# Cross-attention over a long context: context read feature-major, the mean taken out of the weights, keys staged in DRAM, the rescaling factor spread by DMAs

## The chip, the cores and the metric

The kernel runs on one core of a Trainium2 chip. The core has a matrix engine (TensorE, PE in the profile, with PEld for its weight loads), a vector engine (VectorE, DVE), a scalar engine (ScalarE, ACT), a general engine (GpSimd, POOL) and a queue engine that only issues DMAs (SyncE, SP). Each engine works through its own queue in order, and the engines wait for each other by semaphores. The metric is the device time of one execution in microseconds.

## The reference

The model is one layer of a Perceiver: 512 latent rows of 512 features attend to a context of 8192 rows, and a stack of eight blocks and a routed feed-forward layer follow. Only the first part, the cross-attention, is touched by the change. Everything is float32.

```python
def layer_norm(x, g, b):
    mu = jnp.mean(x, axis=-1, keepdims=True)
    var = jnp.var(x, axis=-1, keepdims=True)
    return (x - mu) * jax.lax.rsqrt(var + EPS) * g + b

xn = layer_norm(x, gamma_x, beta_x)          # x: the context, 8192 x 512
ln = layer_norm(latents, gamma_l, beta_l)    # latents: 512 x 512
q = (ln @ Wq).reshape(b, m, h, d)            # 8 heads of 64
kv_x = xn @ Wkv
k_x, v_x = (kv_x[..., :INNER], kv_x[..., INNER:])
kv_l = ln @ Wkv                              # the latents are keys and values too
k_l, v_l = (kv_l[..., :INNER], kv_l[..., INNER:])
k_x = rope_rotate_k(k_x)                     # halves of each head turned by cos and sin of the position
...
k = jnp.concatenate([k_x, k_l], axis=2)      # 8704 keys
v = jnp.concatenate([v_x, v_l], axis=2)
attn = jax.nn.softmax(jnp.einsum('bhid,bhjd->bhij', q * scale, k), axis=-1)
out = jnp.einsum('bhij,bhjd->bhid', attn, v)
out = jnp.transpose(out, (0, 2, 1, 3)).reshape(b, m, INNER) @ Wo
...
x = x + cross_attention(ctx_1024, _layernorm(x), ...)
x = x + eight_blocks(_layernorm(x), ...)
x = x + routed_feed_forward(_layernorm(x), ...)
```

## The kernel before

The attention is computed with keys on the partitions and queries along the free axis. The 8704 keys are cut into 17 blocks of 512: block 0 is the latents themselves, blocks 1 to 16 are the context. A block is four chunks of 128 keys. The eight heads are four pairs.

**From context rows to keys and values.** `fetch_block` loads four row tiles of 128 x 512 and the cos and sin table of the block. `moments_of` (L176, L177, DVE) takes mean and variance of each row, `roots_of` the reciprocal root by three Newton steps on tiles of 4 columns (on POOL from block 3 on), and `centre` (L194, ACT) applies `r*x - r*mean` in place. `transpose_rows` (L218, PE) turns the tiles to features on partitions, 16 transposes a block, and its four evictions (L224, ACT) multiply by gamma and add beta. `keys_of(b, j)` multiplies four feature tiles with 128 columns of the key weights (L231); the weights' columns are permuted so that j even holds first halves of heads and j odd second halves. DVE multiplies the product by cos and sin (L249), POOL combines the halves (L254, L255), and eight DMAs on SP's queue (L262) place the 32-row pieces into two key tiles. `values_of(b, t)` (L231 too) makes the values of one chunk, evicted by ACT (L270).

**From keys to the output.** The work on scores is cut into 24 *units*. A unit is one pair of heads and a run of chunks: 4, 6, 9, 12, 12, then sixteen times 13, then 10, 7, 4. `score` makes two 128 x 512 products of one chunk (pc, L379), ACT copies them out of PSUM (L382), and DVE keeps the running maximum over chunks (mx, L386, L388). At the unit's end `maxima` transposes that maximum (pmx, L397), DVE reduces it and joins it with the pair's earlier maximum (mrow, L401), POOL subtracts old and new (alpha, L406), and ACT takes the exponential (L407): this is the factor by which the pair's earlier output must shrink. `maxima_rows` (mbc, L416) spreads the maximum over the partitions. `shrink` spreads alpha the same way by eight small products (pa, L427), and DVE multiplies the pair's accumulated output and sums with it (L432). `exponentials` subtracts on DVE (L439), takes the exponential on ACT (L440), and POOL adds the chunks up in one buffer (es, L448, L450). `weigh` multiplies with the values (po, L460), `sums` turns es into the denominators (pd, L499), and `gather` (L490) adds both into the pair's output. When a pair is done, `ones_over` multiplies by the reciprocal (L523), and `project` (L483) applies the output weights.

**What sets the order.** PE's order is the program's order, written out by hand (`manual_schedule`). Time is counted in *pairs of steps* d: each d makes the scores of two chunks, and `todo[d]` holds what else PE does in it, sorted by `rank`. A block takes 8 of these d, a unit of 13 chunks 6.5. The other engines and SP's queue are ordered by the framework's scheduler when the program is built. PSUM has five banks shared by scores, projections and transposes (`ps_s`, bufs 5); the score tiles in SBUF have 18 buffers, es has one. `queued(...)` keeps an operation from being put before a given one.

The opening, before d = 0, makes keys and values of block 1 and of block 0 and the queries. The tail projects, adds the residual, and opens the next stage, whose first weights SP loads (L131).

Of the kernel before, what the change touches and what calls it, by code (L numbers as in the profile page):

```python
# [13 lines left out]
PSUM = bass.MemoryType.PSUM  # L14
DRAM = bass.MemoryType.DRAM

P = 128
# [37 lines left out]
def perceiver_kernel(  # L55
    ctx: ExitStack, tc: tile.TileContext, x, cx, wq_x, wkv_x, wo_x, wq, wk, wv, wo, wf1, wf2,
# [81 lines left out]
    xnp = pool("x_feat", 4, stack=xa)  # L138
    cbp = pool("x_rows", 4, stack=xa)
    xpool = pool("xattn", 1, stack=xa)  # L140
    kvp = pool("x_kv", 27, stack=xa)
    sp = pool("x_s", 18, stack=xa)
# [69 lines left out]
    k_sb, v_sb, xT, part, rows_of, trigs = {}, {}, {}, {}, {}, {}  # L212

    def transpose_rows(b, dc, gcol, bcol):
# [4 lines left out]
        xT[b, dc] = xnp.tile([P, BLK], F32, tag="xn", name="xn")  # L219
        scale, shift = (col[:, c + dc : c + dc + 1] for c in (gcol, bcol))  # L220
        if b == 1 and dc % 2:
            nc.vector.tensor_scalar(xT[b, dc], pt, scale, shift, ALU.mult, ALU.add)
        else:
            nc.scalar.activation(xT[b, dc], pt, AF.Identity, bias=shift, scale=scale)  # L224
# [12 lines left out]
    def keys_of(b, j):  # L237
# [37 lines left out]
    def fetch_block(b):  # L275
# [1106 lines left out]
```

## Time and profile before

| | us |
|---|---|
| median of 3 runs (2569.86 to 2571.99) | 2571.08 |
| the profiled execution | 2571.29 |
| its span | 2569.2 |
| PE busy in the span | 2501.5 |
| DVE busy | 1746.6 |
| ACT busy | 1202.3 |
| POOL busy | 1263.4 |

The span is the time from the first to the last recorded instruction; 2.1 us of the execution lie outside it. The granted clock of TensorE was 0.995 on average. A group in the profile is named by line, engine and operation, then what it writes and reads with the shapes; `x` is the count, then busy time and the mean of one in nanoseconds, and behind the bar the idle time of the engine just before such instructions, with what ended it. PE's float32 products are recorded as two instructions each, transposes as one. In the timeline a row is a run of equal instructions: start, length, and in brackets the idle time before it.

### The profile page before, as it was taken

Reading aid. Unit: us, or ns where it says so; the run is one execution under the profiler, and the core shown is the slowest. Engines: PE = TensorE matmul, PEld = TensorE weight load, DVE = VectorE, ACT = ScalarE, POOL = GpSimd, SP = SyncE. Lnnn points to the kernel's source line nnn. Section 1 sums busy time; section 2 is a strip of 40 time slices with the busy share of each in tenths; the row PEclk is TensorE's granted clock in tenths of the full one; section 3 lists DMA queues with packets and bytes.
Section 4 is the critical chain, followed back from the end, with each engine's and each line's share of the span. In section 5 each row is a group of like instructions: output and inputs, shape, how many; then the busy total and the mean of one; then the engine's idle time right before and its main releaser. Section 6 shows DMA issues by size and latency. Waiting matters only on the chain.

```text
span 2569.2 us, 33740 instructions
## 1 busy us (share of the span) xinstructions
PE 2501.5 (97%) x11560; PEld 1471.0 (57%) x11560; DVE 1746.6 (68%) x3680; ACT 1202.3 (47%) x2285; POOL 1263.4 (49%) x1422
## 2 busy tenths in 40 slices
PE   8999999999999999998999999999999999999998
PEld 4433333334333333333588686886868878687764
DVE  4466767766777776886675767757576575766764
ACT  3465656665566665663433415334153441524303
POOL 0255665666567666775144452544525354263512
PEclk9999999999999999998999999999999999999999
DMA  3111111111111111010522223222222323223235
GB/s 134 42 44 52 29 41 42 42 40 43 34 42 41 42 42 42 9 42 17 193 95 93 72 79 106 95 95 70 95 95 90 95 86 97 92 74 99 66 110 203
DMA packets 98380, 187.49 MB, mean 73 GB/s; under 512 B 10336, under 2 KB 10464, under 8 KB 98208
## 3 DMA queue, kind: packets, MB, share of 16 engines
q1 hardware_dynamic: 88496, 167.29, 20.3%
q10 hardware_dynamic: 8688, 15.94, 2.0%
q0 software_dynamic: 1024, 2.10, 0.3%
q8 instruction: 92, 1.51, 0.2%
q14 instruction: 80, 0.66, 0.1%
HBM read 162.22 MB, written 1.05 MB: 64 GB/s over the span
## 4 chain that ended last, share of the span: by engine, by line
PE 78%; DVE 9%; ACT 5%; issue 4%; POOL 2%; DMA 0%; SPq 0%; DVEq 0%; POOLq 0%; ACTq 0%
PE pb L846 14%; PE ps L635 13%; PE pw L730 9%; PE pv L231 7%; PE pk L231 6%; PE ps L730 6%; PE po L460 6%; PE pc L379 6%; DVE sc L439 4%; PE po L1009 4%; ACT sc L382 2%; ACT sc L440 2%; DVE mx L388 1%; PE pt L218 1%; PE pf L939 1%
## 5 line engine op out<-in xcount | busy, mean ns | idle before, releaser
L450 POOL TENSOR_TENSOR es<-es,sc 128x1024 f32<-128x1024 f32 x222 | 526.1, 2370 | 110.5 <-ACT sc L440 99.9
L388 DVE TENSOR_TENSOR mx<-pc,mx 128x512 f32<-128x512 f32 x448 | 283.3, 684 | 186.5 <-ACT sc L382 186.3
L440 ACT ACTIVATE sc<-sc 128x1024 f32<-128x1024 f32 x272 | 288.4, 1065 | 249.2 <-DVE sc L439 238.1
L382 ACT COPY sc<-pc 128x512 f32<-128x512 f32 x544 | 284.4, 600 | 81.3 <-PE pc L379 67.6
L439 DVE TENSOR_TENSOR sc<-sc,mbc 128x1024 f32<-128x1024 f32 x272 | 319.4, 1209 | 3.7 <-PE mbc L416 2.2
L379 PE MATMUL pc<-qT,k 64*128 64x512 f32 x1088 | 290.9, 621 | 5.8 <-DVE sin L249 2.3
L460 PE MATMUL po<-sc,v 128*64 128x512 f32 x1088 | 263.0, 604 | 0.2 <-DVE mx L388 0.2
L231 PE MATMUL pk<-xn,wkv 128*64 128x512 f32 (+1 forms) x856 | 250.6, 604 | 8.2 <-ACT v L270 3.4
L231 PE MATMUL pv<-wkv,xn 128*64 128x512 f32 (+1 forms) x808 | 248.0, 598 | 7.7 <-DVE sin L249 2.6
L379 PEld LDWEIGHTS pc<-qT,k 64*128 64x128 f32 x1088 | 101.4, 186 | 189.0 <-issue 80.9
L1019 ACT ACTIVATE h<-h,col 128x256 f32<-128x256 f32 x192 | 103.9, 577 | 220.5 <-DVE h L779 151.0
L903 ACT ACTIVATE g<-g 128x512 f32<-128x512 f32 x64 | 39.9, 630 | 344.7 <-DVE g L863 218.7
L730 PE MATMUL pw<-curT,cur 128*128 128x256 f32 (+1 forms) x896 | 177.3, 350 | 0.1
L231 PEld LDWEIGHTS pk<-xn,wkv 128*64 128x64 f32 (+1 forms) x856 | 85.0, 153 | 160.8 <-issue 114.1
L231 PEld LDWEIGHTS pv<-wkv,xn 128*64 128x64 f32 (+1 forms) x808 | 86.6, 155 | 150.8 <-issue 110.8
L812 POOL TENSOR_TENSOR sh<-h 128x128 f32<-128x128 f32 x120 | 83.4, 695 | 176.7 <-PE pb L846 172.1
L986 POOL TENSOR_TENSOR y<-qf,y 128x512 f32<-128x512 f32 x32 | 44.5, 1391 | 243.9 <-DVE y L985 243.9
L730 PEld LDWEIGHTS pw<-curT,cur 128*128 128x128 f32 x896 | 150.2, 190 | 16.9 <-DVE curT L723 0.2
L863 DVE TENSOR_TENSOR g<-g,pb 128x256 f32<-128x256 f32 x135 | 50.0, 417 | 159.7 <-PE pb L846 159.2
L717 POOL TENSOR_TENSOR cur<-w 128x256 f32<-128x256 f32 x128 | 93.5, 741 | 118.5 <-DVE g L904 74.9
L460 PEld LDWEIGHTS po<-sc,v 128*64 128x64 f32 x1088 | 73.6, 138 | 135.2 <-issue 120.0
L846 PE MATMUL pb<-tw,sh 128*128 128x256 f32 x540 | 136.2, 379 | 0.0
(220 smaller groups left out, 4639.7 us busy)
## 6 DMA issues: line engine op xcount, KB each, us to landing
w<-in_wf SPq DMA_DIRECT2D x64, 1024.0 KB, 5.2
k<-cos SPq DMA_DIRECT2D x272, 64.0 KB, 2.0
cb<-in_cx SPq DMA_DIRECT2D x62, 256.0 KB, 3.9
row<-in_rows ACTq DMA_DIRECT2D x48, 256.0 KB, 4.7
f<-in_f SPq DMA_DIRECT2D x10, 1024.0 KB, 5.3
tg<-in_trig SPq DMA_DIRECT2D x16, 512.0 KB, 3.6
wk<-in_wk SPq DMA_DIRECT2D x8, 1024.0 KB, 5.2
wq<-in_wq SPq DMA_DIRECT2D x8, 1024.0 KB, 5.1
```

The source lines that it names most:

```text
L231: nc.tensor.matmul(ps[o : o + n, :], lhs(dc)[:, o : o + n], rhs(dc), start=(dc == 0), stop=(dc == DC - 1))
L379: nc.tensor.matmul(pc[h], k_sb[b, p][hs, o : o + P], qT[hs, p, :], start=True, stop=True)
L382: copied[0] = nc.scalar.copy(sc[:, h, :], pc[h])
L388: behind[0] = nc.vector.tensor_tensor(mx[u][:, h, :], pc[h], mx[u][:, h, :], ALU.max)
L439: nc.vector.tensor_tensor(sc, sc, mbc[u], ALU.subtract)
L440: nc.scalar.activation(sc, sc, AF.Exp)
L450: nc.gpsimd.tensor_tensor(es[u], es[u], sc, ALU.add)
L460: nc.tensor.matmul(po[u][h * HD : (h + 1) * HD, :], v_sb[b, p][:, t * P + h * HD : t * P + (h + 1) * HD], scores[u, i][:, h, :], start=(i ...
L635: nc.tensor.matmul(ps[:, t0 : t0 + n], w[:, dc, c0 : c0 + P], xT[:, dc, t0 : t0 + n], start=(dc == 0), stop=(dc == DC - 1),)
L730: nc.tensor.matmul(ps, lhs[:, k], rhs[:, k], start=(k == 0), stop=(k == 1))
L846: nc.tensor.matmul(ps[i], lhs, rhs, start=(q == 0 and i in (1, 2, 6, 5, 4)), stop=(q == self.N - 1 and i in (1, 2, 7, 3, 4)),)
L1019: nc.scalar.activation(h, h, AF.Gelu_apprx_tanh, bias=col[:, c : c + 1])
```

## The change

The context is sent a second time, transposed (`cxt`, features by rows). `fetch_features` loads a block of it as four feature tiles, so blocks 2 to 16 need no `transpose_rows` and no `centre`; the row tiles are still loaded, for their moments only. The layer norm is taken apart:

- The factor r of each row: `spread_roots` writes the 512 reciprocals to DRAM and reads them back on all partitions, and `scale_tokens` multiplies the four feature tiles with them, on POOL (for block 2 half on DVE).
- The mean: with gamma multiplied into the weights and the column's mean taken off (`column_means`, PE; `centre_weights`, DVE), the product of a raw row is the product of its centred row. This is done once, in the opening, when block 1 and block 0 have used the weights as they are.
- The shift beta becomes a bias: `beta_of` multiplies it with the weights, one column at a time. For keys the bias is added in the multiplication by cos and sin; for values it is added at the end, times the sum of the weights, in `ones_over`. Block 0's values are made from `xT - beta` so that the one bias holds for all.

Keys go to DRAM in two tiles per two products (POOL's queue issues these writes from block 2 on) and `load_keys` brings them back for each unit and block, two d ahead, on SP's queue. Alpha's subtraction moves from POOL to DVE; `factor` transposes alpha (PE), takes the exponential (ACT), and writes it to DRAM, from where two DMAs spread it; the units of `spread_here` (21, 22, 23) keep the products of before. The shrinking is put at `end + 4` where the DMAs spread, and stays at `end + 2` in the others. Pools: feature tiles 2 of 8 KB a partition (4 of 2 KB before), key and value tiles 15 (27), 4 tiles of loaded keys, score tiles 19 (18).

```diff
-    xnp = pool("x_feat", 4, stack=xa)
+    xnp = pool("x_feat", 2, stack=xa)
-    kvp = pool("x_kv", 27, stack=xa)
-    sp = pool("x_s", 18, stack=xa)
+    kvp = pool("x_kv", 15, stack=xa)
+    ktp = pool("x_k", 4, stack=xa)
+    sp = pool("x_s", 19, stack=xa)
+    dram = pool("x_dram", 1, DRAM, stack=xa)
...
+        if b > 1:
+            roots[b] = r, None
+            return
...
+    def spread_roots(b):
+        line = dram.tile([TT, P], F32, name=f"r{b}")
+        nc.sync.dma_start(out=line.rearrange("t p -> p t"), in_=roots[b][0])
+        spread[b] = xpool.tile([P, BLK], F32, tag="rbc", name="rbc")
+        nc.sync.dma_start(out=spread[b], in_=line.rearrange("t p -> (t p)").partition_broadcast(P))
+    def scale_tokens(b, dc):
+        x = xT[b, dc]
+        eng = nc.vector if b == 2 and dc % 2 else nc.gpsimd
+        eng.tensor_tensor(x, x, spread[b], ALU.mult)
     def normalizing(b):
-        yield from ((1 + t // 2, moments_of, b, t) for t in range(TT))
+        yield from ((t // 2, moments_of, b, t) for t in range(TT))
-        yield from ((6 + t // 2, centre, b, t) for t in range(TT))
+        if b < 2:
+            yield from ((6 + t // 2, centre, b, t) for t in range(TT))
+        else:
+            yield (4, spread_roots, b)
+            yield from ((6 + dc // 2, scale_tokens, b, dc) for dc in range(DC))
...
-    def transpose_rows(b, dc, gcol, bcol):
+    bias = xpool.tile([P, 2, DC], F32, name="bias")
+    g_d = xpool.tile([P, DC], F32, name="g_d")
+    early = ps_o.tile([P, 2, DC], F32, tag="o", name="early")
+    def transpose_rows(b, dc, dst, gcol, bcol):
-        xT[b, dc] = xnp.tile([P, BLK], F32, tag="xn", name="xn")
-        scale, shift = (col[:, c + dc : c + dc + 1] for c in (gcol, bcol))
+        xT[b, dc] = dst
+        scale = col[:, gcol + dc : gcol + dc + 1]
+        shift = 0.0 if bcol is None else col[:, bcol + dc : bcol + dc + 1]
         if b == 1 and dc % 2:
-            nc.vector.tensor_scalar(xT[b, dc], pt, scale, shift, ALU.mult, ALU.add)
+            nc.vector.tensor_scalar(dst, pt, scale, None, ALU.mult)
+        elif bcol is None:
+            nc.scalar.activation(dst, pt, AF.Copy, scale=scale)
         else:
-            nc.scalar.activation(xT[b, dc], pt, AF.Identity, bias=shift, scale=scale)
+            nc.scalar.activation(dst, pt, AF.Identity, bias=shift, scale=scale)
+    def beta_of(i, j):
+        for dc in range(DC):
+            nc.tensor.matmul(
+                early[:, i, j : j + 1], wkv[:, i, dc, j * P : (j + 1) * P],
+                col[:, C_BX + dc : C_BX + dc + 1], start=(dc == 0), stop=(dc == DC - 1),
+            )
+        nc.vector.tensor_copy(bias[:, i, j : j + 1], early[:, i, j : j + 1])
+    def column_means(i):
+        for dc in range(DC):
+            nc.tensor.matmul(
+                means[:, i, :], g_d[:, dc : dc + 1].to_broadcast([P, P]), wkv[:, i, dc, :],
+                start=(dc == 0), stop=(dc == DC - 1),
+            )
+    def centre_weights(i):
+        for dc in range(DC):
+            w = wkv[:, i, dc, :]
+            nc.vector.scalar_tensor_tensor(
+                w, w, col[:, C_GX + dc : C_GX + dc + 1], means[:, i, :], ALU.mult, ALU.subtract
+            )
     def projected(ps, lhs, rhs):
...
-                nc.vector.tensor_tensor(part[c + str(half)], pk, trigs[b][:, i, :], ALU.mult)
+                nc.vector.scalar_tensor_tensor(
+                    part[c + str(half)], pk, bias[:, 0, j : j + 1], trigs[b][:, i, :], ALU.add, ALU.mult
+                )
-        for p in (j - 1, j):
-            k_sb[b, p] = kv_tile(f"k{b}_{p}")
-            for h in range(2):
-                src = slice((p % 2 * 2 + h) * H2, (p % 2 * 2 + h + 1) * H2)
-                for i, half_of in enumerate((lo, hi)):
-                    o = h * HD + i * H2
-                    nc.sync.dma_start(out=k_sb[b, p][o : o + H2, :], in_=half_of[src, :])
+        k_dr[b, j // 2] = dram.tile([2, P, BLK], F32, name=f"k{b}_{j // 2}")
+        for i, half_of in enumerate((lo, hi)):
+            (nc.gpsimd if b > 1 else nc.sync).dma_start(out=k_dr[b, j // 2][i], in_=half_of)
+    def load_keys(u, b, lo, hi):
+        kt[u, b] = ktp.tile([P, BLK], F32, tag="kt", name=f"kt{u}_{b}")
+        p = units[u][0]
+        for h in range(2):
+            o = (p % 2 * 2 + h) * H2
+            nc.sync.dma_start(
+                out=kt[u, b][h * HD : (h + 1) * HD, lo:hi], in_=k_dr[b, p // 2][:, o : o + H2, lo:hi]
+            )
     def values_of(b, t):
-        projected(pv, lambda dc: xT[b, dc][:, t * P : (t + 1) * P], lambda dc: wkv[:, 1, dc, :])
+        projected(pv, lambda dc: xT[b if b else "v", dc][:, t * P : (t + 1) * P], lambda dc: wkv[:, 1, dc, :])
...
-    def fetch_block(b):
+    def fetch_rows(b):
...
+    def fetch_turns(b):
+    def feature_tiles(b, tiles):
+        for dc in range(DC):
+            xT[b, dc] = tiles[dc]
+    def fetch_features(b):
+        t = xnp.tile([P, DC, BLK], F32, tag="xn", name="xn")
+        nc.sync.dma_start(out=t, in_=cxt[:, (b - 1) * BLK : b * BLK].rearrange("(c p) t -> p c t", p=P))
+        feature_tiles(b, [t[:, dc, :] for dc in range(DC)])
     def normalize_block(b):
...
     def fetch_weights(i):
-    fetch_block(1)
+    fetch_rows(1)
+    fetch_turns(1)
+    spare = {}
+    for b in (1, "v"):
+        spare[b] = []
+        for _ in range(2):
+            t2 = sp.tile([P, 2, T], F32, tag="s", name="xs")
+            spare[b] += [t2[:, h, :] for h in range(2)]
+    fetch_rows(2)
+    fetch_features(2)
+    nc.vector.tensor_scalar(g_d, col[:, C_GX : C_GX + DC], 1.0 / D, None, ALU.mult)
-        transpose_rows(1, dc, C_GX, C_BX)
+        transpose_rows(1, dc, spare[1][dc], C_GX, None)
+        beta_of(0, j)
-    fetch_block(2)
+    fetch_turns(2)
+    own = xnp.tile([P, DC, BLK], F32, tag="xn", name="xl")
-        transpose_rows(0, dc, C_GL, C_BL)
+        transpose_rows(0, dc, own[:, dc, :], C_GL, C_BL)
+        xT["v", dc] = spare["v"][dc]
+        nc.gpsimd.tensor_scalar(xT["v", dc], xT[0, dc], col[:, C_BX + dc : C_BX + dc + 1], None, ALU.subtract)
...
+    normalize_block(2)
+    means = ps_m.tile([P, 2, T], F32, tag="m", name="means")
+    column_means(0)
+    centre_weights(0)
+    column_means(1)
+    for j in range(DC):
+        beta_of(1, j)
-    normalize_block(2)
+    centre_weights(1)
...
-        for dc in range(DC):
-            if dc == 2 and b > 2:
-                at(begin, values_of, b - 1, TT - 1)
-            at(begin, transpose_rows, b, dc, C_GX, C_BX)
-        at(begin, *((fetch_block, b + 1) if b < NBLK else (fetch_last,)))
-        pieces = *((keys_of, j) for j in range(2)), (values_of, 0), *((keys_of, j) for j in (2, 3)), (values_of, 1), (values_of, 2)
+        if b < NBLK:
+            at(max(-1, begin - 4), fetch_rows, b + 1)
+            at(begin + 1, fetch_features, b + 1)
+            at(begin + 6, fetch_turns, b + 1)
+        else:
+            at(begin, fetch_last)
+        pieces = *((keys_of, j) for j in range(2)), (values_of, 0), *((keys_of, j) for j in (2, 3)), *((values_of, t) for t in (1, 2, 3))
-    at(begin + 8 * gap, values_of, NBLK, TT - 1)
     def score(u, i):
...
-            nc.tensor.matmul(pc[h], k_sb[b, p][hs, o : o + P], qT[hs, p, :], start=True, stop=True)
+            nc.tensor.matmul(pc[h], kt[u, b][hs, o : o + P], qT[hs, p, :], start=True, stop=True)
...
-            nc.gpsimd.tensor_tensor(a, mrow[p], new, ALU.subtract)
-            nc.scalar.activation(a, a, AF.Exp)
+            nc.vector.tensor_tensor(a, mrow[p], new, ALU.subtract)
     def maxima_rows(u):
...
+    def factor(u):
+        a = alpha[u]
+        if u in spread_here:
+            nc.scalar.activation(a, a, AF.Exp)
+            return
+        pa = bank("pa")
+        nc.tensor.transpose(pa[: 2 * TT, :P], a, ident)
+        turned = xpool.tile([2 * TT, P], F32, tag="turned", name="turned")
+        nc.scalar.activation(turned, pa[: 2 * TT, :P], AF.Exp)
+        line = dram.tile([2 * TT, P], F32, name=f"al{u}")
+        nc.sync.dma_start(out=line, in_=turned)
+        abc[u] = xpool.tile([P, T], F32, tag="abc", name="abc")
+        for h in range(2):
+            nc.sync.dma_start(
+                out=abc[u][h * HD : (h + 1) * HD, :],
+                in_=line[h * TT : (h + 1) * TT, :].rearrange("c p -> (c p)").partition_broadcast(HD),
+            )
     def shrink(u):
-        pa = bank("pa")
-        for qc in range(TT):
-            for h in range(2):
-                c = h * TT + qc
+        if u in spread_here:
+            abc[u] = bank("pa")
+            for c in range(2 * TT):
+                h, qc = divmod(c, TT)
-                    pa[h * HD : (h + 1) * HD, qc * P : (qc + 1) * P],
+                    abc[u][h * HD : (h + 1) * HD, qc * P : (qc + 1) * P],
-            oT[p], oT[p], pa.unsqueeze(1).to_broadcast([P, 2, T]), ALU.mult
+            oT[p], oT[p], abc[u].unsqueeze(1).to_broadcast([P, 2, T]), ALU.mult
     def exponentials(u, i, late=False):
...
+    spread_here = {u for u, n in enumerate(size) if u > NPAIR and n < 12}
     def project(ps, tiles):
...
-        nc.vector.tensor_tensor(outT[p], oT[p][:, 0, :], pb, ALU.mult)
+        nc.vector.scalar_tensor_tensor(
+            outT[p], oT[p][:, 1, :], bias[:, 1, p : p + 1], oT[p][:, 0, :], ALU.mult, ALU.add
+        )
+        nc.vector.tensor_tensor(outT[p], outT[p], pb, ALU.mult)
...
-            at(end[u] + 2, shrink, u)
+            at(end[u] + 1, factor, u)
+            at(end[u] + (2 if u in spread_here else 4), shrink, u)
+        for b in range(units[u][1] // TT, (units[u][2] - 1) // TT + 1):
+            c0, c1 = max(units[u][1], b * TT), min(units[u][2], (b + 1) * TT)
+            at(
+                max(-1, (end[u] * 2 + 1 - n + c0 - units[u][1]) // 2 - 2),
+                load_keys, u, b, (c0 - b * TT) * P, (c1 - b * TT) * P,
+            )
...
-    rank = {maxima_rows: 0, maxima: 2, exponentials: 3, shrink: 4, ones_over: 4, weigh: 5, sums: 6, late_weigh: 6.5, late_maxima: 7, late_exponentials: 8}
+    rank = {maxima_rows: 0, factor: 0.5, maxima: 2, exponentials: 3, shrink: 4, ones_over: 4, weigh: 5, sums: 6, late_weigh: 6.5, late_maxima: 7, late_exponentials: 8}
-        whole = {maxima, maxima_rows, transpose_rows, sums_by_query}
+        whole = {maxima, maxima_rows, sums_by_query}
...
-        "x": a["x"].reshape(T, D), "cx": a["ctx_1024"].reshape(CTX, D),
+        "x": a["x"].reshape(T, D), "cx": a["ctx_1024"].reshape(CTX, D), "cxt": a["ctx_1024"].reshape(CTX, D).T,
```

More of the change, by code (lines that the diff above doesn't have):

```diff
@@ L14 @@
 PSUM = bass.MemoryType.PSUM
+DRAM = bass.MemoryType.DRAM
 DRAM = bass.MemoryType.DRAM
@@ L55, in perceiver_kernel @@
 def perceiver_kernel(
-    ctx: ExitStack, tc: tile.TileContext, x, cx, wq_x, wkv_x, wo_x, wq, wk, wv, wo, wf1, wf2,
+    ctx: ExitStack, tc: tile.TileContext, x, cx, cxt, wq_x, wkv_x, wo_x, wq, wk, wv, wo, wf1, wf2,
     ctrl, f1, f2, cols, rows, consts, trig, out,
@@ L211, in perceiver_kernel @@
     H2 = HD // 2
-    k_sb, v_sb, xT, part, rows_of, trigs = {}, {}, {}, {}, {}, {}
-    def transpose_rows(b, dc, gcol, bcol):
+    k_dr, v_sb, xT, part, rows_of, trigs, spread, kt = {}, {}, {}, {}, {}, {}, {}, {}
+    bias = xpool.tile([P, 2, DC], F32, name="bias")
+    g_d = xpool.tile([P, DC], F32, name="g_d")
+    early = ps_o.tile([P, 2, DC], F32, tag="o", name="early")
+    def transpose_rows(b, dc, dst, gcol, bcol):
         tiles = rows_of[b]
@@ L367, in perceiver_kernel @@
             at(begin + e, f, *a)
-    at(begin + 8 * gap, values_of, NBLK, TT - 1)
     pieced = set(todo)
-    scores, mx, mrow, alpha, mbc, es, po = {}, {}, {}, {}, {}, {}, {}
+    scores, mx, mrow, alpha, mbc, es, po, abc = {}, {}, {}, {}, {}, {}, {}, {}
     def score(u, i):
@@ L546, in perceiver_kernel @@
             at(last + 2, ones_over, u)
-    rank = {maxima_rows: 0, maxima: 2, exponentials: 3, shrink: 4, ones_over: 4, weigh: 5, sums: 6, late_weigh: 6.5, late_maxima: 7, late_exponentials: 8}
-    for d in range(max(todo) + 1):
+    rank = {maxima_rows: 0, factor: 0.5, maxima: 2, exponentials: 3, shrink: 4, ones_over: 4, weigh: 5, sums: 6, late_weigh: 6.5, late_maxima: 7, late_exponentials: 8}
+    for d in range(min(todo), max(todo) + 1):
         behind[1] = behind[0]
-        for s in steps[2 * d : 2 * d + 2]:
+        for s in steps[2 * d : 2 * d + 2] if d >= 0 else ():
             score(*s)
-        whole = {maxima, maxima_rows, transpose_rows, sums_by_query}
+        whole = {maxima, maxima_rows, sums_by_query}
         halved[0] = not any(f in whole for f, a in todo.get(d, []))
```

## The prediction

> **What bounds the kernel now.** I read the page, a table of stretches, PE's timeline, and the waits by engine. All changed work lies in the attention stage, which ends at 1231 us.
>
> ```profile
> 0.00:86.30 86.30, 75.52 (x192) 35.75 (x192) 28.79 (x100) 23.36 (x53) 5.75 (x11) 1.00 0.33 111
> 86.30:600.00 513.70, 500.88 (x2185) 195.04 (x2184) 360.43 (x524) 311.31 (x562) 304.79 (x276) 1.00 0.14 41
> 600.00:1120.00 520.00, 507.73 (x2252) 193.61 (x2250) 382.91 (x543) 322.96 (x575) 340.79 (x261) 1.00 0.13 38
> 1120.00:1231.00 111.00, 93.18 (x450) 40.20 (x446) 75.44 (x111) 47.24 (x70) 59.74 (x28) 0.92 0.06 20
> ```
>
> Columns: length, then busy time of PE, PEld, DVE, ACT, POOL, then clock and DMA. From 86 to 1120 us PE is busy 1009 of 1034 us, DVE 743, ACT 634, POOL 646. The clock is full. So PE's own instructions set the pace, and what is taken from PE counts unless another wait takes its place. PE's timeline (start, length):
>
> ```profile
> 204.08 1.09 PE L416 MATMUL mbc<-ident,mrow 128*128 128x128 f32 x8
> 205.01 1.04 PE L218 MATMUL pt<-ident,cb 128*128 128x128 f32 x8
> 205.88 3.60 PE L231 MATMUL pv<-wkv,xn 128*128 128x512 f32 x8
> 209.32 1.04 PE L218 MATMUL pt<-ident,cb 128*128 128x128 f32 x8
> 210.28 1.08 PE L460 MATMUL po<-sc,v 128*64 128x512 f32 x4
> ...
> 642.14 2.02 PE L379 MATMUL pc<-qT,k 64*128 64x512 f32 x8
> 647.03 3.65 PE L231 MATMUL pk<-xn,wkv 128*64 128x512 f32 x16 [2.88 <-ACT v L270]
> 650.52 1.04 PE L427 MATMUL pa<-ident,alpha 128*64 128x128 f32 x16
> 651.39 1.03 PE L460 MATMUL po<-sc,v 128*64 128x512 f32 x4
> ```
>
> Lengths overlap, so I price by start to start: a block's 16 transposes take 0.87+0.96 = 1.83 us here, a unit's spreading of alpha (pa) 0.87. The idle 2.88 us comes from ACT, and ACT's waits say why:
>
> ```profile
> ACT alpha L407 <- POOL alpha L406: 72.5, 17, 8.7
> ACT sc L382 <- PE pc L379: 67.6, 58, 5.4
> ```
>
> The exponential of alpha stands in ACT's queue until POOL, busy with the rsqrt chain, has subtracted. Score copies queue behind it.
>
> Prices used for the other engines:
>
> ```profile
> L450 POOL TENSOR_TENSOR es<-es,sc 128x1024 f32<-128x1024 f32 x222 | 526.1, 2370 | 110.5 <-ACT sc L440 99.9
> L448 POOL TENSOR_TENSOR es<-sc 128x1024 f32<-128x1024 f32 x23 | 54.5, 2369 | 140.7 <-PE pd L499 67.9 <-ACT sc L440 39.1 <-ACT xn L224 26.5
> L254 POOL TENSOR_TENSOR cos<-cos,sin 128x512 f32<-128x512 f32 x30 | 38.5, 1282 | 0.0
> L432 DVE TENSOR_TENSOR x_sb<-x_sb,pa 128x1024 f32<-128x1024 f32 x10 | 12.1, 1213 | 2.4 <-PE pa L427 2.4
> L1286 POOL DMA_DIRECT2D it<-it x32: 538/538/752, 2534.8 to 2558.6; - x32
> ```
>
> **The change, part by part.** The sum runs against the profiled execution, 2571.29 us (span 2569.2 and 2.1 around it); the median of the runs, 2571.08, is the same within 0.01%. I call under 0.2% (5.1 us) no change: that is about what this measurement can tell.
>
> 1. *Transposes of blocks 2 to 16 go* (the context arrives feature-major). 15 x 16 of them; start to start over PE's timeline they sum to 31.9 us (15 x 1.83 = 27.5 is the floor). All on PE: **-31.9**. Also gone are 4 evictions at 0.796 us and 4 centrings at 0.839 per block on ACT, 98 us beside PE; they return in term 6.
>
> 2. *The factor is spread by DMAs* in 17 of 20 units (the last three keep matmuls): -17 x 0.87 = -14.8, and 17 transposes at 0.13 (192 pmx transposes take 24.1 us) = +2.1: **-12.7**.
>
> 3. *Mean out of the weights.* 8 products of 512 columns, 16 instructions; 16 such took 6.87 us in the opening: +6.9. The second half's sums wait for DVE's four centrings of the first half: 4 x 0.72 us (DVE scalar_tensor_tensor from PSUM, L990) = +2.9. The shifts: 32 products of one column, 64 instructions. No such row; the nearest, 128x128 fp32 weights with 128 columns (L635), takes 5.40 us for 40 = 0.135, so +8.6; floor 0.054 each (pa), 3.5; ceiling one weight load each, 0.19, 12.2. The opening is PE in a row with no cover: **+18.4**.
>
> 4. *Stage start.* DVE's four centrings of the value weights (2.9 us) stand before the first maxima while the transposes that filled PE there are gone: **+1.5** (0 to 3).
>
> 5. *Bias into the rotation*: 120 DVE operations go from 0.686 to 0.722 us, +4 us beside PE; the final multiplies gain four of about 0.7 to 1.0, of which the last stands while PE spreads the reciprocal: 0, at worst +1.
>
> 6. *Waits that go.* PE's listed waits in the stage sum to 39.5 us, and the scores take 285 us where 136 steps at 1.92 make 261: some 63 us in which PE waits for banks. Alpha's subtraction moves to DVE, so ACT's 72.5 us of waiting go, and with them its 98 us of work. How much PE gets back is unknown: 0 to 30. I take a sixth of 63, **-10**, as most of those waits name DVE.
>
> 7. *Factor round trip.* New chain: DVE alpha, PE transpose, ACT, a DMA to DRAM, two DMAs back, then DVE's multiply. In the built order that multiply stands only 2 or 3 score steps after alpha in nine of 17 units (4, 5, 6, 9, 11, 13 to 15, 17). Two landings at 2.0 us (key DMAs), issues at 0.58 and ACT's queue make some 9 us after PE's transpose; DVE has about 6 us of work before it. So it stands up to 3 us, with maxima and subtractions behind it. In the trace a DVE pause of 6.9 us (before 641.69) cost PE 2.88, so: **+4** (0 to 27).
> [...]
>
> 8. *POOL.* Added per block: 4 scalings at 1.28, 4 DMA issues (0.54 each for 64 KB; four times the rows at most 2.15), and a wait for the spread reciprocal of 0 to 5.5 us (two landings and issues). Gone: two small operations and alpha. What matters is the loop per unit (13 steps, about 49 us): PE's pd frees es, POOL adds 12 times, PE's pd waits for the last. Between first and last es the built order holds at most 12 x 2.37 + 15 x 0.29 + 4 x 1.28 + 2 x 1.28 = 40.5 us (units 8, 9, 13, 14) and 2 issues: 41.6 to 50.3 with both unknowns. Elsewhere 31 to 36. So the loop holds, with little room in five units: **+5** (0 to 25).
>
> 9. *Keys through DRAM.* SP drops 272 issues of 0.58 us and gains 164 loads, which now queue behind waits for POOL's reciprocal. Loads go two pairs of steps (15 us) ahead. Tightest are units 18 and 7, 3 and 3.5 pairs from key product to use: DVE 1.4, POOL 2.6 and backlog, issue, write, load at 2.0 each, about 12 of 23 us. **+2** (0 to 10).
> [...]
>
> 10. *First layer's weights* now stand on SP behind w_c, which waits for the last attention output (about 1213 in today's times): issues of 0.45+2.59+1.07, then a landing of 5.2, about 1223 against first use at 1231.6. Cost 0; without that cover up to 5.
>
> Sum: -31.9 -12.7 +18.4 +1.5 -10 +4 +5 +2 = -23.7: **2548 us**.
>
> **Rivals.**
> *A. POOL becomes the bound* (slower). If an issue costs 2.15 us and the reciprocal's round trip stands in POOL's queue, the loop of term 8 passes 49 us in the full units, score copies wait for es buffers (19 instead of 18), and key writes and SP's loads fall behind in other units too. It decides once POOL's delays cost PE over 29 us beyond term 8's five, some 2 us a unit. Price 35 to 60: 2583 to 2608. For it: POOL's work goes from 646 to about 740 of 1000 us. Against: POOL idles 110 us before es today.
> *B. DVE takes the bound over.* Its wait at the multiply is served in full (27 instead of 4) and nothing of term 6 returns: 2548+23+10 = 2581, or half of both, 2565. For it: DVE is 74 of 100 busy on 10 to 13 us of new work, with PE's banks freed by it. Against: PE lost under half of today's pauses.
> *C. ACT's relief is worth more*: term 6 at 30, terms 7 to 9 near 3: 2520.
> *D. PE's released time is not released*: if removed transposes only filled waits for banks, term 1 halves: 2564. Against: only 2.0 us idle stand before them.
>
> **How the numbers follow.** Forecast as summed (2535 to 2562): 0.47. C (2515 to 2535): 0.18. B or D half way (2562 to 2577): 0.15. A, or B in full (over 2577): 0.20. Faster takes the first two and a fifth of the third, 0.67; same 0.10; slower 0.23. The range leaves a tenth at each end: 2518 to 2590.
>
> **What would show it.** Right: no pt rows after the opening; PE's opening about 18 us longer; pa in three units only; no ACT wait on alpha; PE near 97% busy. Wrong: pd rows waiting for es by tens of us, DVE idle before the multiply on DMA by more than 50 us in sum, pc rows waiting for a key load, or one-column products above 0.19 us each.

## The result: 6.8% slower

The changed kernel takes 2745.26 us (median of 4 runs, 2743.20 to 2747.91) against 2570.5 us for the kernel before: a ratio of 1.068, 95% interval 1.066 to 1.070. That is 175 us more, 155 us beyond the upper end of the forecast range. The profiled execution took 2747.91 us, with a span of 2746.1.

All but a few of those microseconds are lost before the first layer. Its first product starts at 1404.1 us instead of 1231.6. These are the stretches of the changed kernel (length, then busy time of PE, PEld, DVE, ACT, POOL, then granted clock and DMA share):

```profile
0.00:108.00 108.00, 93.27 (x272) 47.49 (x272) 37.38 (x117) 20.33 (x49) 15.36 (x17) 0.98 0.37 130
108.00:600.00 492.00, 425.00 (x1674) 154.85 (x1674) 318.21 (x450) 230.81 (x428) 308.52 (x271) 0.92 0.22 69
600.00:1120.00 520.00, 440.99 (x1710) 156.12 (x1708) 327.84 (x465) 232.25 (x427) 319.93 (x262) 0.90 0.22 68
1120.00:1404.00 284.00, 247.07 (x1078) 96.47 (x1076) 212.78 (x292) 143.42 (x234) 177.52 (x99) 0.95 0.12 41
```

PE was 97.6% busy in the attention stage; now it is 86% busy (866 of 1012 us from 108 to 1120), and its clock has fallen to 0.90 to 0.92. No other engine took over: DVE and POOL are about 64% and 62% busy there. So nothing here is bound by work. Everybody waits. The opening is 21.7 us longer (108.0 instead of 86.3). For the rest of the stage, up to the first layer's first product, PE's timeline added up from start to start (86.3 to 1231.6 us before, 108.0 to 1404.1 after) gives this ledger:

- removed products (transposes, and 17 of 20 spreadings of the factor, less 17 new transposes): -43.1 us
- PE's listed idle time: 182.95 instead of 42.44 us, **+140.5 us**
- the same products as before, but slower: +53.4 us, of which the scores take 23.6 and the key products 15.4
- sum: +150.8, the growth of the stage from the end of the opening to the first layer.

Whom do they wait for? These are the waits from 108 to 1404 us, of PE, POOL and DVE (total, times, longest):

```profile
PE pc L470 <- DVE sin L301: 45.8, 9, 11.1
PE pd L609 <- DVE mx L479: 38.7, 4, 19.6
PE pc L470 <- DVE mx L479: 25.4, 7, 7.4
PE pk L283 <- DVE sin L301: 24.5, 3, 10.9
...
POOL xn L211 <- DMA rbc<-r: 87.3, 7, 17.0
...
POOL xn L211 <- issue: 32.0, 3, 11.9
...
DVE cos L301 <- DMA k<-cos: 87.5, 10, 14.2
DVE x_sb L541 <- DMA abc<-al: 49.2, 5, 24.2
DVE oT L541 <- DMA abc<-al: 45.0, 6, 13.4
```

PE names DVE, but DVE itself waits for DMAs: at the rotation (L301) until a key write has read the buffer that it wants to overwrite, and at the multiply with the factor (L541) until the spread factor has landed. The key writes are issued by POOL, and POOL stands at the scaling (L211) until the spread reciprocal has landed. The profile names that DMA in eight of these waits over the whole run (103.6 us, seven of them in the lines above), "issue" in three and an instruction of PE in four. But POOL waits before the first scaling of all 15 blocks, and all 15 scalings start 2.8 to 5.6 us after the load of the reciprocal was issued, so all 15 are the same wait: 184.7 us, 12.3 per block. One stall, the longest of PE, shows how these hang together. SP's queue comes first, from 726 to 758 us (start, length):

```profile
726.52 0.38 SPq L204 DMA_DIRECT2D r<-ny  x1
737.20 0.33 SPq L206 DMA_DIRECT2D rbc<-r  x1
751.24 1.05 SPq L319 DMA_DIRECT2D kt<-k  x2
752.39 0.40 SPq L521 DMA_DIRECT2D al<-turned  x1
756.48 1.12 SPq L524 DMA_DIRECT2D abc<-al  x2
```

Then the same time on POOL, ACT, DVE and PE:

```profile
726.29 0.20 POOL L85 TENSOR_TENSOR ny<-ny 128x4 f32<-128x4 f32 x1
726.44 2.35 POOL L559 TENSOR_TENSOR es<-es,sc 128x1024 f32<-128x1024 f32 x1
740.67 2.50 POOL L211 TENSOR_TENSOR xn<-xn,rbc 128x512 f32<-128x512 f32 x2 [11.88 <-issue]
...
747.85 1.15 POOL L312 DMA_DIRECT2D k<-cos  x2
...
730.68 0.27 ACT L519 ACTIVATE turned<-pa 8x128 f32<-8x128 f32 x1 [0.34 <-PE pa L517]
...
759.93 1.22 DVE L541 TENSOR_TENSOR x_sb<-x_sb,abc 128x1024 f32<-128x1024 f32 x1 [24.24 <-DMA abc<-al]
...
761.90 1.98 PE L609 MATMUL pd<-es,ones 128*64 128x512 f32 x4 [19.60 <-DVE mx L479]
```

Read it as one chain. The reciprocal is ready at 726.5 and its write is issued at once, but its load is issued only at 737.2, when the write has landed: 10.3 us in which SP stands. POOL has one addition of other work and then stands 11.9 us. Its next key write goes out behind that, at 747.9. SP's key load, next in its queue, waits for this write and is issued at 751.2. Behind that load stands the write of the factor, whose data ACT had finished at 730.95: it waited 21 us in SP's queue for things that it does not need. The multiply starts 7.5 us after that write is issued. DVE stands 24 us at its multiply, and PE stands 19.6 us.

### The profile page after: what moved, and what is told of

Same layout as the page of the kernel before. It is cut to its first block, busy times and chain, and to the rows that moved or that the text cites. A ratio compares the mean times of both kernels' runs of the same rounds, so it can differ in the third digit from the quotient of the medians.

```text
span 2746.1 us, 33126 instructions
## 1 busy us (share of the span) xinstructions
PE 2532.5 (92%) x11217; PEld 1462.3 (53%) x11217; DVE 1795.4 (65%) x3722; ACT 1122.7 (41%) x2165; POOL 1372.3 (50%) x1496
## 4 chain that ended last, share of the span: by engine, by line
PE 56%; DVE 5%; DMA 3%; issue 2%; ACT 2%; POOL 2%; SPq 0%; DVEq 0%; ACTq 0%; POOLq 0%
PE pb L966 13%; PE ps L755 11%; PE pw L850 8%; PE ps L850 6%; PE po L1129 3%; PE po L569 3%; PE pc L470 3%; PE pv L283 2%; PE pk L283 2%; DVE sc L548 1%; DMA al<-turned 1%; PE pf L1059 1%; POOL es L559 1%; PE pt L1048 1%; DMA r<-ny 1%
## 5 line engine op out<-in xcount | busy, mean ns | idle before, releaser
L470 PE MATMUL pc<-qT,kt 64*128 64x512 f32 x1088 | 315.5, 650 | 73.1 <-DVE sin L301 45.8
L283 PE MATMUL pk<-xn,wkv 128*64 128x512 f32 (+1 forms) x792 | 236.1, 635 | 36.2 <-DVE sin L301 24.5
L470 PEld LDWEIGHTS pc<-qT,kt 64*128 64x128 f32 x1088 | 109.3, 194 | 271.1 <-issue 111.0
L283 PE MATMUL pv<-wkv,xn 128*64 128x512 f32 (+1 forms) x816 | 224.4, 612 | 6.3 <-DVE sin L301 5.8
L1023 ACT ACTIVATE g<-g 128x512 f32<-128x512 f32 x64 | 39.7, 628 | 345.2 <-DVE g L983 219.1
L283 PEld LDWEIGHTS pk<-xn,wkv 128*64 128x64 f32 (+1 forms) x792 | 78.1, 158 | 187.0 <-issue 146.3
L211 POOL TENSOR_TENSOR xn<-xn,rbc 128x512 f32<-128x512 f32 x58 | 75.2, 1322 | 184.7 <-DMA rbc<-r 103.6
L283 PEld LDWEIGHTS pv<-wkv,xn 128*64 128x64 f32 (+1 forms) x816 | 72.6, 149 | 148.9 <-issue 107.7
```

What stands on the lines that cost most here:

```text
L283: nc.tensor.matmul(ps[o : o + n, :], lhs(dc)[:, o : o + n], rhs(dc), start=(dc == 0), stop=(dc == DC - 1))
L470: nc.tensor.matmul(pc[h], kt[u, b][hs, o : o + P], qT[hs, p, :], start=True, stop=True)
```

## The experiments

The name of a theory in the expectations is explained in the first of them. Times are medians; the ratio is to the kernel before in the same session, with its 95% interval. The idle time is the sum of PE's waits in the profile from 60 us to the first layer's first product, that product's own wait left out.

| kernel | time, us | ratio | PE's listed idle time before the first layer, us |
|---|---|---|---|
| before | 2570.5 to 2573.0 | 1 | 41.8 |
| changed kernel | 2745.26 | 1.068 (1.066 to 1.070) | 185.1 |
| reciprocal spread by PE | 2627.67 | 1.022 (1.020 to 1.023) | 81.8 |
| factor spread by PE in all units | 2706.64 | 1.052 (1.050 to 1.054) | 136.4 |
| both spread by PE | 2572.99 | 1.0005 (0.9996 to 1.0015) | 38.8 |
| reciprocal written in rows of 512 bytes | 2601.79 | 1.010 (1.007 to 1.013) | 74.4 |
| scalings later | 2644.51 | 1.029 (1.027 to 1.031) | 110.3 |
| reciprocal's DMAs issued by POOL | 2763.32 | 1.074 (1.072 to 1.075) | 188.0 |
| multiply later | 2693.34 | 1.047 (1.046 to 1.049) | 143.6 |
| scalings and multiply later | 2575.47 | 1.0014 (1.0004 to 1.0023) | 61.2 |
| rows of 512 bytes, factor by PE | 2557.03 | 0.994 (0.992 to 0.995) | 34.5 |
| rows of 512 bytes, multiply later | 2550.05 | 0.991 (0.990 to 0.993) | 42.2 |
| the same, both column means first | 2543.97 | 0.989 (0.987 to 0.990) | 39.7 |
| before, alpha subtracted on DVE | 2551.39 | 0.991 (0.990 to 0.993) | 29.9 |

### Take the round trips away, one and then both

**The reciprocal on PE.** The two DMAs go; four products with the identity and an ACT copy spread the reciprocal, one step of pairs later.

```diff
-        line = dram.tile([TT, P], F32, name=f"r{b}")
-        nc.sync.dma_start(out=line.rearrange("t p -> p t"), in_=roots[b][0])
+        pr = bank("pr")
+        for t in range(TT):
+            nc.tensor.matmul(
+                pr[:, t * P : (t + 1) * P], roots[b][0][:, t : t + 1].to_broadcast([P, P]), ident,
+                start=True, stop=True,
+            )
         spread[b] = xpool.tile([P, BLK], F32, tag="rbc", name="rbc")
-        nc.sync.dma_start(out=spread[b], in_=line.rearrange("t p -> (t p)").partition_broadcast(P))
+        nc.scalar.copy(spread[b], pr)
...
-            yield (4, spread_roots, b)
+            yield (5, spread_roots, b)
```

> The reciprocal deviations are spread over the partitions by four PE products and one ACT copy, one step later than the DMAs were issued; no reciprocal goes through DRAM. Theory R (the reciprocal's round trip is the root: POOL stands 103.6 us in eight waits on it and 32 us more, and SP stands 8 to 11 us per block between its write and its load, with key loads and the factor's DMAs behind): the POOL waits at the scaling fall under 20 us, DVE's 94 us at the shrink fall under 30, and the time is 2580 to 2620, for 15 x 0.5 us more on PE. Theory F (the factor's own round trip is the root): POOL's wait goes but DVE's 94 us stay, and the time stays over 2690. Theory L (POOL has too much work, or keys through DRAM are late by themselves): over 2650.

2627.67 us: 118 us of the 175 come back, a little less than theory R foresaw. POOL waits 9.3 us at the scaling, once, and DVE's waits at the multiply fall from 94.2 to 37.1 us (20.2 + 16.9) although nothing in the factor's own path was touched. So more than half of the factor's lateness came from what stood ahead of it.

**The factor on PE.**

```diff
-    spread_here = {u for u, n in enumerate(size) if u > NPAIR and n < 12}
+    spread_here = {u for u, n in enumerate(size) if u >= NPAIR}
```

> The factor is spread by eight PE products in all 20 units, as before the change; the reciprocal still goes through DRAM. Theory R: DVE's 94 us at the shrink go, but POOL's 104 us at the scaling and DVE's 87 us at the rotation for the key writes stay: 2690 to 2740. Theory F: 2600 to 2640. Theory L: over 2690 too.

2706.64 us, as R said (L gave the same range; the next run separates the two): 39 us come back. POOL still waits 179.1 us at the scaling, and DVE's waits for key writes rise from 87.5 to 98.7.

**Both on PE.**

> Both are spread by PE; only keys still go through DRAM. Theories R and F: 2570 to 2600, PE over 95% busy in the stage. Theory L: over 2650, with DVE still waiting some 80 us for key writes. The difference to the kernel with the reciprocal alone on PE is the price of the factor's round trip where the reciprocal's is gone: near 0 by R (PE pays 0.87 us per unit for it, so it may be up to 13 us slower), 60 or more by F.

2572.99 us, no different from the kernel before that a measurement can tell. Keys still go through DRAM here, so theory L falls. The price of the factor's trip beside a healthy reciprocal is 2627.67 - 2572.99 = 55 us. That is near F's figure, not R's "near 0": the factor's trip is a second loss of its own, not only an echo of the first.

### Keep the round trips, change their pieces or their place

**Long rows.** The reciprocal is transposed by PE to [4, 128] first, so it leaves as four rows of 512 bytes instead of 512 pieces of 4 bytes.

```diff
-        nc.sync.dma_start(out=line.rearrange("t p -> p t"), in_=roots[b][0])
+        pr = bank("pr")
+        nc.tensor.transpose(pr[:TT, :P], roots[b][0], ident)
         spread[b] = xpool.tile([P, BLK], F32, tag="rbc", name="rbc")
+        nc.scalar.copy(spread[b][:TT, :P], pr[:TT, :P])
+        line = dram.tile([TT, P], F32, name=f"r{b}")
+        nc.sync.dma_start(out=line, in_=spread[b][:TT, :P])
...
-            yield (4, spread_roots, b)
+            yield (5, spread_roots, b)
```

> The reciprocal is transposed by PE first, so that it is written to DRAM in four rows of 512 bytes instead of 512 pieces of 4 bytes; the load back is the same. If the small pieces make the 8.2 us between the write's issue and the load's, this gap falls to 2 to 3 us and the time to 2600 to 2660; if any round trip in SP's order costs this, the gap stays over 6 us and the time over 2700.

2601.79 us. SP's queue in that run:

```profile
390.46 0.27 SPq L208 DMA_DIRECT2D r<-rbc  x1
391.68 0.37 SPq L349 DMA_DIRECT2D tg<-in_trig  x1
392.14 0.37 SPq L209 DMA_DIRECT2D rbc<-r  x1
```

From the end of the write's issue to the load's issue passes 1.4 us (median of 14 blocks; one took 7.4), with another DMA in between here; in the changed kernel it was 8.1 us, up to 12.2. Same 2 KB, same queue: writing it as 512 pieces of 4 bytes instead of four rows made the difference. POOL's wait for the landing falls from 184.7 to 19.0 us. The kernel's gain of 143 us is not all due to the pieces, because the transpose also puts the scalings later in POOL's order. Why this run is 26 us faster than the one with the reciprocal on PE is explained in part: there `pr` takes 14.5 us of PE time instead of 2.6. The rest was not taken apart.

**Scalings later**, with round trip and pieces untouched.

```diff
-        eng.tensor_tensor(x, x, spread[b], ALU.mult)
+        with tc.issue_after(adds[0]) if b > 2 else nullcontext():
+            eng.tensor_tensor(x, x, spread[b], ALU.mult)
...
-            yield from ((6 + dc // 2, scale_tokens, b, dc) for dc in range(DC))
+            yield from ((7, scale_tokens, b, dc) for dc in range(DC))
...
-            nc.gpsimd.tensor_tensor(es[u], es[u], sc, ALU.add)
+            adds[0] = nc.gpsimd.tensor_tensor(es[u], es[u], sc, ALU.add).ins
```

> As the changed kernel, round trips and their pieces untouched; only the four scalings stand later in POOL's order, behind the additions of the step after, so that POOL has some 15 to 20 us of other work between its last rsqrt instruction and the first scaling. If POOL's standing in its own order is what costs (104 and 32 us of its waiting): that waiting falls under 15 us and the time to 2600 to 2650, the rest being DVE's waits at the shrink. If SP's standing between the reciprocal's write and its load costs by itself, the same 8 us gap stays on SP and the time over 2680.

2644.51 us: 101 us come back from an order alone. In this run SP still stands 8.1 us (median) between the reciprocal's write and its load. But POOL waits at the scaling only once, for block 2 in the opening, whose order the edit leaves, and DVE's waits for key writes fall from 87.5 to 23.4; the multiply still waits 72.5:

```profile
DVE oT L542 <- DMA abc<-al: 46.4, 6, 14.1
DVE x_sb L542 <- DMA abc<-al: 26.1, 5, 13.1
DVE cos L302 <- DMA k<-cos: 23.4, 5, 11.2
POOL xn L212 <- DMA rbc<-r: 16.1, 1, 16.1
```

**The reciprocal's DMAs on POOL's queue.** This separates POOL's standing from SP's.

```diff
-        nc.sync.dma_start(out=line.rearrange("t p -> p t"), in_=roots[b][0])
+        nc.gpsimd.dma_start(out=line.rearrange("t p -> p t"), in_=roots[b][0])
...
-        nc.sync.dma_start(out=spread[b], in_=line.rearrange("t p -> (t p)").partition_broadcast(P))
+        nc.gpsimd.dma_start(out=spread[b], in_=line.rearrange("t p -> (t p)").partition_broadcast(P))
```

> As the changed kernel, but the reciprocal's write and load are issued by POOL instead of SP. SP no longer stands for them; POOL stands as before, now at the load's issue. If SP's standing is what makes the factor late: DVE's 94 us at the shrink fall under 40 and the time to 2660 to 2700. If POOL's standing is what counts (it holds the key writes, and SP's key loads and the factor behind them): 2725 to 2760, and the waits at the shrink stay over 60 us.

2763.32 us, a little over the upper of the two. SP no longer stands for the reciprocal, and still DVE waits 81.3 us at the multiply (48.0 + 33.3) and 112.5 for key writes. So SP's own standing for the reciprocal is not the root. What holds SP, as in the stall shown above, is the key load that waits for a key write, which waits in POOL's order. This run also lists the landing of the write in 4-byte pieces: 9.0 us from its issue (8.0 to 9.8). POOL, which now issues the load, waits 106.3 us for it in 15 waits, 9.0 us at most.

**Multiply later**, two pairs of score steps, behind that step's maxima.

```diff
-            at(end[u] + (2 if u in spread_here else 4), shrink, u)
+            at(end[u] + (2 if u in spread_here else 6), shrink, u)
...
-        nc.vector.tensor_tensor(
-            oT[p], oT[p], abc[u].unsqueeze(1).to_broadcast([P, 2, T]), ALU.mult
-        )
+        with nullcontext() if u in spread_here else tc.issue_after(behind[0].ins):
+            nc.vector.tensor_tensor(
+                oT[p], oT[p], abc[u].unsqueeze(1).to_broadcast([P, 2, T]), ALU.mult
+            )
```

> As the changed kernel, reciprocal in 4-byte pieces; only the multiply with the factor stands two pairs of score steps later, behind that step's maxima. If DVE's 94 us there are a second loss of their own: they fall under 15 us and the time to 2690 to 2715, near the run with the factor by PE (2707). If they only took the place of waits for POOL: over 2725.

2693.34 us: 52 us come back, and no wait of DVE for the factor is left in the profile. The waits for key writes grow from 87.5 to 119.8 us: part of the time only moved to the next wait.

**Both later.**

> Both moves together, scalings and multiply later, the reciprocal still in 4-byte pieces through SP. If late use is all that both round trips need: 2548 to 2558, as the run with long rows and a late multiply (2550). If SP's 8 us per block cost by themselves through the key loads behind them: 2565 to 2600.

2575.47 us. The two moves together give 170 us, 17 more than the two alone (101 + 52). The pieces and queues of the round trips are those of the changed kernel, and the loss against the kernel before is down to 4 us. So most of it came from instructions that wait for the trips and stand early in engines that execute in order. The time still falls into the second of the two ranges: 25 us more than the next run, whose reciprocal goes out in rows of 512 bytes. DVE waits 34.5 us for key writes here and 8.8 us there. The two runs also differ in where the scalings stand in POOL's order, so whether the small pieces cost this through SP's order, or the later scalings do by delaying the key products, was not separated.

**Long rows and a late multiply.**

> As the kernel with the reciprocal in rows of 512 bytes (2602), but the multiply with the factor stands two pairs of score steps later and, in DVE's order, behind the maxima of its step. If the factor's round trip costs only where its landing is late for DVE (44 us of DVE's waiting in that run): DVE's waits at the shrink fall under 10 us and the time to 2545 to 2562, below the kernel before. If the DMAs cost in another way (SP's order, late key loads): over 2580.

2550.05 us, faster than the kernel before by 0.9%. No wait for the factor remains.

**Long rows, factor by PE.**

> The reciprocal goes through DRAM in rows of 512 bytes, the factor is spread by PE in all units. The run with both on PE gave 2573 and paid some 14.5 us of PE time for the reciprocal's products. Theory R (the small pieces of the reciprocal's write are the root, a round trip with long rows is harmless): 2558 to 2568. If any round trip that SP and POOL wait for costs, 2575 to 2600.

2557.03 us, a microsecond under what R foresaw. This also prices the factor's trip at its best: sent by DMA with a late multiply it saves 7.0 us, although PE's products for it (`pa`) go from 25.5 to 6.3 us. (In the kernel before they took 17.7; why they take longer in this run was not looked into.) Some 12 us are given back elsewhere; the last section names a candidate.

### Two terms of the sum

**Alpha on DVE, in the kernel before.**

```diff
-            nc.gpsimd.tensor_tensor(a, mrow[p], new, ALU.subtract)
+            nc.vector.tensor_tensor(a, mrow[p], new, ALU.subtract)
```

> The kernel before with one edit: the subtraction of the two maxima rows for alpha is made on DVE instead of POOL. My term 6 (ACT's 72.5 us of waiting for POOL go, PE gets back a part): 2555 to 2567. The rival that this waiting is hidden: 2569 to 2573.

2551.39 us against 2573.04: 21.7 us from one instruction's engine, more than either theory said: PE's idle time falls by 11.9 us and the scores take 6.2 us less. ACT's waits for alpha in the stage, which were 72.5 us with a longest of 8.7:

```profile
ACT alpha L407 <- DVE alpha L406: 42.8, 16, 5.4
```

**Column means of both halves first.**

```diff
 column_means(0)
-    centre_weights(0)
     column_means(1)
+    centre_weights(0)
```

> As the run with long rows and the late multiply, with the column means of both halves formed before the first half is centred. If PE's 2.8 us wait for DVE in the opening is only a matter of this order, the wait goes and the time falls by 2 to 3 us against that run; if DVE's centring is late for the first scores instead, the time stays.

2543.97 us, 6.1 less than the run that it starts from (2 to 3 were expected) and the fastest of all: 1.1% under the kernel before. PE in the opening of the changed kernel, and then of this one:

```profile
78.99 3.60 PE L265 MATMUL means<-wkv,g_d 128*128 128x512 f32 x8
85.41 5.40 PE L265 MATMUL means<-wkv,g_d 128*128 128x512 f32 x8 [2.82 <-DVE wkv L274]
```

```profile
76.10 7.03 PE L268 MATMUL means<-wkv,g_d 128*128 128x512 f32 x16
```

The wait of 2.82 us goes, and with it the slow products after it: eight took 5.40 us behind the pause, at a granted clock of 0.68, and 3.60 before it. That makes 4.6; the other 1.5 us are not explained.

## Why the prediction was wrong

*Term 8 failed, and with it the whole forecast.* It bounded POOL's wait for the spread reciprocal by "0 to 5.5 us (two landings and issues)", from the 2.0 us landing of the key DMAs, whose rows are 2 KB long. The stall above had 11.9 us, and all 15 blocks had 5.9 to 17.0, 12.3 in the mean. The write alone, from the end of its issue, kept the load back 8.1 us in the median, against 1.4 us in the run that writes the same 2 KB in rows of 512 bytes instead of 4-byte pieces. The term has no row of a write in such pieces and took the 2.0 us of another shape. An unknown that no row shows should have widened the bound, not been dropped. And the term then asked only whether POOL's *work* fits its loop ("the loop holds"). It did hold as work: 62% busy. The waiting was what did not fit. Moving the scalings gives back 101 us, where the term had +5 (0 to 25).

*Term 7 failed in its bound.* "Some 9 us after PE's transpose" counted landings and issues, but not what stands ahead of the factor in SP's queue. In the stall shown, that was 21 us of the way. Priced by the run that moves the multiply, it is 52 us instead of 4 (0 to 27). Its exchange of 6.9 us of DVE for 2.88 of PE rests on one row, and that row names ACT (`v`, L270) as what PE waited for, not DVE; in the stall shown, 24.2 us of DVE went with 19.6 of PE.

*Term 9 looked at the wrong end.* It followed keys from product to use; in the changed kernel PE never stands for a key load. What came late was the release of the rotation's buffers, which are free only when POOL's key write has read them: DVE waits 87.5 us there, 8.8 when POOL is on time.

*The three were priced as if they were independent.* They share POOL's and SP's orders: a late reciprocal delays the key write, this delays the key load, this delays the factor. Rival A described this mechanism in part ("the reciprocal's round trip stands in POOL's queue", "key writes and SP's loads fall behind") and was given 35 to 60 us and, together with rival B in full, a share of 0.20. That part was right. But POOL did not become the bound (62% busy), and a DMA issue did not cost the 2.15 us that the rival needed (0.56 in the median). Its price was a third to a fifth of the 175, from the same 5.5 us and without the factor and DVE at the end of the chain.

*Term 6 had the right mechanism and half the size:* -10 was forecast; 21.7 us was measured for alpha's move alone, without the rest of ACT's relief that the term also counted.

*What held.* Term 1: no transpose rows after the opening, -31.9. Term 2: `pa` and its transposes make 6.5 us instead of 17.7, -11.2 (forecast -12.7). Term 3: the opening grew by 21.7 us (forecast 18.4); the wait was 2.82 us (2.9), the one-column products are 0.10 us each (0.135), and eight products behind that wait came 1.8 us slower. Term 5: the rotation takes 0.74 us (0.722). Term 10: PE's first layer products have no wait for a weight load.

The run with long rows and a late multiply gave 2550, close to the 2548 of the forecast, but that is not the forecast come true: term 6 was too small by 12 us, and the factor's DMAs saved 7 us where 12.7 were counted.

Of the signs of being wrong, one came as named: DVE idle on the factor's DMA over 50 us (94.2). `pd` rows did stand by tens of us, but 38.7 of it behind DVE and 9.4 behind the additions of es. Of the signs of being right, PE near 97% busy did not come (86%).

## What to carry to other kernels

Price a moved round trip by its landing *in its own shape*, and then ask of each of its waits what else stands behind it in that engine's order and in that queue; here a wait of 12.3 us per block, on an engine that is busy 62% of the time, cost 101 us, more than the change removed. Place the instruction that needs the result so late in its engine's order that other work covers the whole trip: this alone gave back 170 us, and left 25 between it and the run with long rows. And where several new waits share a queue, price the chain and not the waits.

## What the runs showed of the hardware

**A long pause cost PE twice here.** Behind each of the 19 longest pauses of PE in the stage of the changed kernel (3.34 to 19.6 us) the granted clock of the next 3 us was 0.50 to 0.53. The changed kernel, around a pause of 10.9 us, by stretches and on PE's timeline:

```profile
205.00:214.00 9.00, 9.00 (x40) 2.72 (x36) 3.98 (x6) 5.77 (x13) 5.96 (x5) 1.00 0.21 58
214.00:225.00 11.00, 0.08 (x3) 0.11 (x4) 1.63 (x3) 1.28 (x3) 10.90 (x8) 0.59 0.13 48
225.00:231.00 6.00, 6.00 (x18) 1.99 (x20) 4.46 (x7) 2.11 (x2) 4.72 (x3) 0.61 0.12 44
231.00:240.00 9.00, 9.00 (x42) 2.95 (x40) 4.98 (x7) 3.76 (x9) 7.60 (x7) 1.00 0.32 117
```

```profile
207.57 3.65 PE L283 MATMUL pk<-xn,wkv 128*64 128x512 f32 x16
...
224.92 6.00 PE L283 MATMUL pk<-xn,wkv 128*64 128x512 f32 x16 [10.92 <-DVE sin L301]
```

The same sixteen instructions take 3.65 us at a clock of 1.00 and 6.00 us at 0.61. Behind shorter pauses it varied: the clock of the next 3 us was 0.65 behind the 2.82 us in the opening, and 1.00 behind one of 2.17 us (at 1213.1) and, in the kernel before, behind the 2.88 us of the exchange that the prediction used (a DVE pause of 6.9 us costs PE 2.88). So that exchange left the lower clock out. In the trace's clock records PE works 119 us of the stage at a clock of 0.50, and 18 us in the kernel before. If a product at 0.50 takes twice as long as at 1.00, as the sixteen above fit their clock (3.65 / 6.00 = 0.61), half of the 101 us between the two makes some 51 of the 53 us of slower products, an estimate.

**The multiply with the factor in SBUF took longer beside POOL.** The multiply with the factor in PSUM (before) and in SBUF (the changed kernel), by groups:

```profile
L432 DVE TENSOR_TENSOR oT<-oT,pa 128x1024 f32<-128x1024 f32 x10 | 12.1, 1210 | 0.0
```

```profile
L541 DVE TENSOR_TENSOR oT<-oT,abc 128x1024 f32<-128x1024 f32 x9 | 17.5, 1945 | 45.0 <-DMA abc<-al 45.0
L541 DVE TENSOR_TENSOR x_sb<-x_sb,abc 128x1024 f32<-128x1024 f32 x8 | 16.0, 2005 | 49.2 <-DMA abc<-al 49.2
```

The 17 multiplies take 33.5 us instead of 20.6. With the factor in PSUM all 20 took 1.19 to 1.22 us, though POOL was at work beside 19 of them. In the changed kernel the six beside which POOL has no work take 1.22 to 1.23 us each; each of the eleven others, 1.43 to 3.59 us long, ends 1.08 or 1.09 us after the end of an operation of POOL that ran beside it. In the run with long rows and a late multiply they take 38.3 (1.21 to 4.51 each), and a subtraction of 128x8 for alpha, 0.16 us at its shortest, takes 3.63 (DVE, then POOL at that time):

```profile
471.31 3.63 DVE L500 TENSOR_TENSOR alpha<-mrow 128x8 f32<-128x8 f32 x1
...
467.66 4.95 POOL L214 TENSOR_TENSOR xn<-xn,rbc 128x512 f32<-128x512 f32 x4
472.58 2.33 POOL L563 TENSOR_TENSOR es<-es,sc 128x1024 f32<-128x1024 f32 x1
```

It ends at 474.94, when POOL's addition ends (474.91). Against the factor in PSUM, the 17 multiplies of the changed kernel lost 12.9 us of DVE time. That is a likely part of why the factor's DMAs save so little; no run takes it alone.
